# Layer-0 projections as two column tiles of 64 channels, and a new order of a unit's steps, in a two-layer attention kernel

## The chip, the cores and the metric

The kernel runs on one core of a Trainium2 chip. The metric is the device time of one execution in microseconds (us). Before the change the median of three runs is 2491.27 us, with 2487.93 us the lowest and 2491.57 us the highest. About 0.2% (5 us) is what a measurement of this kernel can tell from no change.

## The reference

`x` has shape (8, 512, 32, 32): 8 images, 512 channels, 1024 tokens, all float32. Layer 0 is a group norm, eight-head attention over the 1024 tokens and an output projection with a residual. Layer 1 projects to values, attends among the 256 tokens of greatest norm and writes these back before its own output projection. The change touches layer 0 alone, whose core is:

```
h    = group_norm(x, gn_w, gn_b).reshape(B, C, N)
qkv  = einsum('oc,bcn->bon', qkv_w, h) + qkv_b        # q, k, v: 8 heads x 64 channels
attn = softmax(einsum('bhdi,bhdj->bhij', q, k) * 64**-0.5)
out  = einsum('bhij,bhdj->bhdi', attn, v).reshape(B, C, N)
x1   = x + einsum('oc,bcn->bon', proj_w, out) + proj_b
```

## The kernel before

**Units.** Layer 0 works in 64 units: a unit `t` is one pair of heads (`p = t // 2`, of 4 pairs per image) and one half of the query tokens (`hf = t % 2`, 512 of 1024). In a unit, keys go in eight blocks `j` of 128. `scores` (L947) multiplies q and k for both heads: each head has a contraction of 64 channels, so the two heads stand in the two row halves of the TensorE array and run at the same time. The raw scores are copied to SBUF by ScalarE (`keep`, L955); VectorE follows the maximum (`highest`, L961), turns it into one number per query (`turn`, `negate`), which goes out to DRAM and comes back spread over all partitions (`nb`); ScalarE puts that into PSUM (`spread`, L1002), VectorE adds it (`shift`, L1006), ScalarE takes the exponential (L1009), GpSimd sums the eight exponentials (`add`, L1014), and `values` (L1022) multiplies by v. In `values` each head gives 64 output channels, so the two heads stand in the two *column* halves of the array. `total` (L1037) sums over partitions in four column tiles of 32; `take` (L1045) copies, `invert` (L1051) takes the reciprocal, which again goes through DRAM, and `divide` (L1064) scales the unit's output.

**Fills.** Between these steps stand up to five "fills" per unit: other matrix products of 8 or 16 TensorE passes that go through one PSUM bank (pool `ps_g`, one buffer), each emptied by an "empty" before the next fill may start. Fills 0 and 1 project q or k of a later pair (L750), fill 2 projects v (L771), fills 3 and 4 are the output projection of the image before (L789), in four units of each image from the second on. `side(t)` lists them. All of these use the whole 128 x 128 array.

**Order.** Every engine works its instructions in the order written. The order inside a unit is the word list `SLOT`, read word by word by the loop at the end of `layer0`: a name and number is a step and its block; each `+` means that the step belongs to the next unit, each `-` to the one before. So one pass of the loop holds steps of up to four units. `FIRST_STEPS` places the first products before the loop is full; the last entries of `side` place the start of layer 1 among the last units; `norms` hangs the next image's group norm on certain words of `SLOT`.

**Buffers that tie the order.** Scores and `total` share two PSUM buffers (`ps_s`), so a score product waits until the one two before it has been copied and compared. The product with v has one buffer (`ps_a`): the first `values` step of a unit waits for `divide` of the unit before. Exponentials go through 14 buffers (`ep`).

A float32 product is two TensorE passes for each matmul of the program, so a fill of four matmuls shows as eight in the trace.

Of the kernel before, what the change touches and what calls it, by code (L numbers as in the profile page):

```python
# [18 lines left out]
P = 128  # L19
B = 8  # L20
C = 512
N = 1024
CT = C // P
NB = N // P
NH = 2
HALF = N // NH
HEADS = 8
HD = 64
NPAIR = HEADS // 2
# [16 lines left out]


SLOT = """
fill1 max5+ sc3+ spread empty1 max2+ sub1 exp1 sub0 sub2 sc6+ fill0 exp0 keep3+ div- val1 sub5
add1 max3+ val0 exp2 max6+ exp5 val2 sub6 add2 empty0 keep6+ sub3 val5 sub7 exp6 fill3+ add5  # L50
sc4+ exp3 sub4 empty3+ add6 exp7 sc7+ max4+ exp4 keep4+ add3 max7+ fill2+ keep7+ turn+ neg+
sc0++ add7 sc1++ val3 keep0++ val6 val4 val7 keep1++ add4 den max1++ empty2+ fill4 take inv
sc5++ sc2++ keep5++ empty4 keep2++
"""


# [62 lines left out]
def attention_then_topk_attention(  # L119
# [18 lines left out]
    nc = tc.nc  # L138
# [469 lines left out]
    def layer0():  # L608
        with ExitStack() as st:
# [19 lines left out]
            hs = {0: load_x(0)}  # L629
# [27 lines left out]
            vs, qs, ks, os = {}, {}, {}, {}  # L657
# [73 lines left out]
            def norms(t, name, j):  # L731
                for b in {t // (NPAIR * NH) + 1, (t + 4) // (NPAIR * NH) + 1}:
                    at = t - (b - 1) * NPAIR * NH
                    if 0 < b < B:
# [3 lines left out]
                        for step, *which in todo:  # L738
                            step(b, *which)


            def project(p, which, hf):

                b, hp = divmod(p, NPAIR)
                all_ = (qs, ks)[which]
                ot = which * CT + hp

                def fill(pq):
                    for k in range(CT):
                        nc.tensor.matmul(  # L750
                            pq, wqkv[:, k, ts(ot, P)], hs[b][:, k, ts(hf, HALF)],
                            start=(k == 0), stop=(k == CT - 1),
                        )

                def empty(pq):
                    if p not in all_:
                        all_[p] = qk_tile("qk"[which], p % 2, f"{'qk'[which]}_{p}")
                    nc.scalar.activation(
                        all_[p][:, ts(hf, HALF)], pq, AF.Identity, bias=bqkv[:, ot : ot + 1],
                    )  # L760

                return fill, empty

            def v_tokens(m, part):

                b, hm = divmod(m, NPAIR // 2)

                def fill(pv):
                    for j in range(2):
                        for k in range(CT):  # L770
                            nc.tensor.matmul(  # L771
                                pv[:, ts(j, 2 * P)], hs[b][:, k, ts(2 * part + j, P)],
                                wqkv[:, k, 2 * C + hm * 2 * P : 2 * C + (hm + 1) * 2 * P],
                                start=(k == 0), stop=(k == CT - 1),
                            )

                def empty(pv):
                    if part == 0:
                        vs[m] = vp.tile([P, NB, 2 * P], F32, tag="v", name=f"v_{m}")
                    nc.scalar.copy(  # L780
                        vs[m][:, ts(part, 2), :], pv.rearrange("p (a c) -> p a c", c=2 * P)
                    )

                return fill, empty

            def project_out(b, mt, hf):
                def fill(po):
                    for k in range(CT):
                        nc.tensor.matmul(  # L789
                            po, wp[:, k, ts(mt, P)], os[b * NPAIR + k][:, ts(hf, HALF)],  # L790
                            start=(k == 0), stop=(k == CT - 1),
                        )

                def empty(po):
                    xr = resid.pop((b, mt, hf))
                    nc.vector.scalar_tensor_tensor(
                        xr, po, pb[:, mt : mt + 1], xr, ALU.add, ALU.add,
                    )
                    nc.sync.dma_start(x1_dram[b][:, mt, ts(hf, HALF)], xr)

                return fill, empty
# [39 lines left out]
            def side(t):  # L841

                todo = []
                p, hf = divmod(t, NH)
                b, at = divmod(t, NPAIR * NH)
                m, part = divmod(t, 2 * NH)
                if hf == 0 and p + 1 < PAIRS:
                    todo += [project(p + 1, 1, h) for h in (1, 0)]
                if hf == 1 and p + 2 < PAIRS:
                    todo += [project(p + 2, 0, h) for h in (1, 0)]  # L850
                if m + 1 < PAIRS // 2:
                    todo.append(v_tokens(m + 1, part))
                if b and 1 <= at <= CT:
                    todo += [project_out(b - 1, at - 1, h) for h in range(NH)]
                if t == 0:
                    todo[2:] = [v_tokens(0, 1), project(1, 0, 0), project(1, 0, 1)]
                if t == 1:
                    todo.append(v_tokens(1, 0))
                if 2 <= t <= 3:
                    todo.append((bias_row, bias_columns)[t - 2]())  # L860

                if t == UNITS - 4:
                    todo.insert(2, turned_values(0))
                if t == UNITS - 3:
                    todo = [joint(0), turned_values(3), turned_values(2), turned_values(1), joint(3)]
                if t == UNITS - 2:
                    todo = [token_values(1), token_values(0), joint(2), joint(1), token_rows(0)]
                if t == UNITS - 1:
                    todo = [
                        token_rows(1), token_values(4), token_values(3), token_values(2),  # L870
                        project_out(B - 1, 0, 0),
                    ]
                return todo

# [294 lines left out]
            with tc.manual_schedule(engines=ORDERED):  # L1169
                for c in range(CT):  # L1170
                    norm_stats(0, c)
                mean_sum(0, ps_g.tile([P, HALF], F32, tag="g", name="pm_0"))
                mean_take(0)
                spread_of(0)
                variance_sum(0, ps_g.tile([P, HALF], F32, tag="g", name="pv_0"))
                variance_take(0)
                norm_factors(0)
                for c in range(CT):
                    norm_apply(0, c)

                FIRST_STEPS = {
                    (-2, "sc", 1): [v_tokens(0, 0)],
                    (-2, "sc", 2): ["empty", project(0, 0, 1)],
                    (-1, "sc", 6): ["empty", v_tokens(0, 2)],
                    (-1, "sc", 7): ["empty"],
                    (-1, "empty", 2): [v_tokens(0, 3)],
                    (-1, "keep", 2): ["empty"],
                }
                pending = []

                def first(step):
                    if step == "empty":
                        end, pt = pending.pop(0)
                        end(pt)
                    else:
                        pool, tag = ((ps_g, "g"), (ps_a, "av"))[len(firsts) % 2]
                        firsts.append(step)
                        pt = pool.tile([P, HALF], F32, tag=tag, name=f"first_{len(firsts)}")
                        step[0](pt)
                        pending.append((step[1], pt))  # L1200

                firsts = []
                for step in (
                    project(0, 1, 0), project(0, 0, 0), "empty", project(0, 1, 1), "empty", "empty",
                ):
                    first(step)
                for t in range(-max(ahead for _, ahead, _ in order), UNITS + 1):
                    if t == -2:
                        hs[1] = load_x(1)
                    if t == 2:  # L1210
                        constants()
                    for name, ahead, j in order:
                        late = name in ("den", "take", "inv", "div") and t + ahead == UNITS - 1
                        if 0 <= t + ahead < UNITS and not late:
                            STEPS[name](t + ahead, j)
                        for step in FIRST_STEPS.get((t, name, j), []):
                            first(step)
                        norms(t, name, j)
                        if name == "div":
                            loads(t)  # L1220
                        if t == UNITS - 1 and (name, j) == ("fill", 1):
                            also(token_rows(2))
                    if t == UNITS - 1:
                        begin_layer1()
                finish()
# [48 lines left out]
```

## Time and profile before

| | |
|---|---|
| median of the runs | 2491.27 us |
| the profiled execution's own time | 2489.56 us |
| its span (first to last instruction) | 2487.9 us |
| TensorE (PE) busy | 2437.7 us, 98% |
| VectorE (DVE) busy | 1963.3 us, 79% |
| ScalarE (ACT) busy | 1414.8 us, 57% |
| GpSimd (POOL) busy | 1160.7 us, 47% |
| mean granted TensorE clock | 0.999 |

Busy TensorE time is the union of its passes, whose ends are modelled; a pass overlaps the next one's start. So what a pass costs is read from the distance of two starts, not from its duration. The weight loads (PEld) run beside the passes. Layer 0 fills the first 2020 us of the span, layer 1 the rest.

### The profile page before, as it was taken

The numbers are of one execution on the slowest core, as the hardware profiler recorded it, in microseconds if no ns is written. First come the engines' busy times: TensorE is split into PE (matmuls) and PEld (weight loads), VectorE is DVE, ScalarE is ACT, GpSimd is POOL, SyncE is SP. The second block draws the span as 40 slices with busy tenths as digits, with TensorE's granted clock in tenths as the row PEclk, the third lists the DMA queues.
The fourth block names the chain that finished last, engine by engine and source line by source line (L and its number), as shares of the span: only waits on it lengthen the run. The fifth ranks groups of instructions, "written<-read, shape, count | busy, mean of one in ns | idle before, by whom it ended". The sixth has DMA issues, their size and how long they took to land. (4 is left out here: it accounts for less than half of the span.)

```text
span 2487.9 us, 27088 instructions
## 1 busy us (share of the span) xinstructions
PE 2437.7 (98%) x9164; PEld 1076.4 (43%) x9164; DVE 1963.3 (79%) x2946; ACT 1414.8 (57%) x1828; POOL 1160.7 (47%) x557
## 2 busy tenths in 40 slices
PE   7999999999999999999999999999999999999998
PEld 3434444444444444444444444444433345555554
DVE  4789987998898889888988898888777566666683
ACT  2567755665666566655765676567656533333421
POOL 0555644665465555545664565455555501111122
PEclk9999999999999999999999999999999999999999
DMA  3002011111211121112011201111213343566553
GB/s 142 15 26 73 30 56 51 69 35 56 84 31 43 56 79 41 43 60 77 26 47 56 77 26 49 59 39 35 89 52 106 123 161 136 209 211 240 188 198 106
DMA packets 108234, 205.24 MB, mean 82 GB/s; under 512 B 19114, under 2 KB 19370, under 8 KB 108096
## 3 DMA queue, kind: packets, MB, share of 16 engines
q1 hardware_dynamic: 82432, 159.95, 19.0%
q10 hardware_dynamic: 18144, 31.48, 3.4%
q0 software_dynamic: 7520, 12.09, 1.7%
q8 instruction: 72, 1.18, 0.2%
q14 instruction: 66, 0.54, 0.1%
HBM read 146.29 MB, written 69.73 MB: 87 GB/s over the span
## 5 line engine op out<-in xcount | busy, mean ns | idle before, releaser
L1014 POOL TENSOR_TENSOR es<-es,e 128x1024 f32<-128x1024 f32 x384 | 912.0, 2375 | 30.1
L955 ACT COPY e<-sc 128x1024 f32<-128x1024 f32 x512 | 505.6, 1013 | 389.4 <-PE sc L947 241.3
L1006 DVE TENSOR_TENSOR e<-e,ns 128x1024 f32<-128x1024 f32 x512 | 594.0, 1212 | 2.0 <-ACT ns L1002 2.0
L1014 POOL TENSOR_TENSOR es<-e,e 128x1024 f32<-128x1024 f32 x64 | 152.0, 2375 | 884.8 <-ACT e L1009 884.8
L1009 ACT ACTIVATE e<-e 128x1024 f32<-128x1024 f32 x512 | 529.1, 1055 | 31.6 <-DVE e L1006 9.8
L961 DVE TENSOR_TENSOR high<-sc,high 128x1024 f32<-128x1024 f32 x384 | 468.9, 1221 | 90.0 <-ACT e L955 50.3
L947 PE MATMUL sc<-q,k 64*128 64x512 f32 x2048 | 510.4, 616 | 5.3 <-ACT e L955 3.2
L1022 PE MATMUL av<-e,v 128*64 128x512 f32 x2048 | 469.4, 600 | 3.5 <-ACT e L1009 2.0
L750 PE MATMUL g<-x,wqkv 128*128 128x512 f32 x992 | 458.8, 605 | 3.4 <-ACT v L780 1.7
L947 PEld LDWEIGHTS sc<-q,k 64*128 64x128 f32 x2048 | 175.3, 185 | 283.6 <-issue 151.3
L750 PEld LDWEIGHTS g<-x,wqkv 128*128 128x128 f32 x992 | 178.3, 189 | 274.8 <-issue 229.9
L1022 PEld LDWEIGHTS av<-e,v 128*64 128x64 f32 x2048 | 136.1, 137 | 320.6 <-issue 257.5
L771 PE MATMUL g<-wqkv,x 128*128 128x256 f32 x976 | 227.0, 386 | 1.3 <-DVE pb L834 1.3
L789 PE MATMUL g<-o,wp 128*128 128x512 f32 x456 | 210.9, 605 | 0.8
L771 PEld LDWEIGHTS g<-wqkv,x 128*128 128x128 f32 x976 | 180.4, 190 | 69.7 <-issue 43.3
L1051 DVE RECIPROCAL rs<-rs 128x256 f32<-128x256 f32 x64 | 112.1, 1751 | 68.4 <-ACT rs L1045 68.4
L534 POOL DMA_INDIRECT V<-sa,at x64 | 64.2, 1003 | 155.2 <-DMA sa<-att 52.7
L789 PEld LDWEIGHTS g<-o,wp 128*128 128x128 f32 x456 | 81.9, 189 | 118.2 <-issue 91.3
L309 PE MATMUL b_pv<-w,x 128*128 128x512 f32 x256 | 114.1, 592 | 0.0
L405 PE MATMUL b_pp<-w,selT 128*128 128x512 f32 x256 | 112.5, 593 | 0.8 <-ACT selT L396 0.7
L961 DVE TENSOR_TENSOR high<-sc,e 128x1024 f32<-128x1024 f32 x64 | 78.1, 1220 | 37.5 <-ACT e L955 37.5
L363 POOL DMA_INDIRECT sel<-sx,who x16 | 16.1, 1007 | 191.0 <-DMA out_dram<-y 72.1
(177 smaller groups left out, 1993.6 us busy)
## 6 DMA issues: line engine op xcount, KB each, us to landing
nb<-negd SPq DMA_DIRECT2D x128, 256.0 KB
x<-in_x_dram SPq DMA_DIRECT2D x32, 512.0 KB
ri<-rsd SPq DMA_DIRECT2D x128, 128.0 KB
sx<-xT ACTq DMA_DIRECT2D x64, 256.0 KB
xr<-in_x_dram SPq DMA_DIRECT2D x58, 256.0 KB
x1d<-xr SPq DMA_DIRECT2D x58, 256.0 KB
sv<-V ACTq DMA_DIRECT2D x56, 256.0 KB
y<-x1d SPq DMA_DIRECT2D x48, 256.0 KB
```

The source lines that it names most:

```text
L309: nc.tensor.matmul(pv, x1[b][k][:, ts(j, P)], w["vo"][:, k, :], start=(k == 0), stop=(k == CT - 1),)
L405: nc.tensor.matmul(pp, tiles["selT", b][:, k, ts(rb, P)], w["qk"[which]][:, k, :], start=(k == 0), stop=(k == CT - 1),)
L750: nc.tensor.matmul(pq, wqkv[:, k, ts(ot, P)], hs[b][:, k, ts(hf, HALF)], start=(k == 0), stop=(k == CT - 1),)
L771: nc.tensor.matmul(pv[:, ts(j, 2 * P)], hs[b][:, k, ts(2 * part + j, P)], wqkv[:, k, 2 * C + hm * 2 * P : 2 * C + (hm + 1) * 2 * P], start ...
L789: nc.tensor.matmul(po, wp[:, k, ts(mt, P)], os[b * NPAIR + k][:, ts(hf, HALF)], start=(k == 0), stop=(k == CT - 1),)
L947: nc.tensor.matmul(sc[:, hh, :], ks[p][r, ts(j, P)], qs[p][r, ts(hf, HALF)], start=True, stop=True,)
L955: nc.scalar.copy(raw[t, j], banks["s", t, j])
L961: nc.vector.tensor_tensor(high[t], banks["s", t, j], raw[t, 0] if j == 1 else high[t], ALU.max)
L1006: nc.vector.tensor_tensor(raw[t, j], raw[t, j], high[t], ALU.add)
L1009: nc.scalar.activation(raw[t, j], raw[t, j], AF.Exp, scale=QK_SCALE)
L1014: nc.gpsimd.tensor_add(sums[t], raw[t, 0] if j == 1 else sums[t], raw[t, j])
L1022: nc.tensor.matmul(avs[t][HD * hh : HD * hh + HD, :], vs[p // 2][:, j, (p % 2) * P + HD * hh : (p % 2) * P + HD * hh + HD], e[:, hh, :], s ...
```

## The change

1. A helper `product` replaces the plain matmul in `project`, `v_tokens` and `project_out`. It issues each product twice, once for output channels (rows of the PSUM bank) 0 to 63 and once for 64 to 127, with 64 columns of weights each. The moving operand and the sums are the same; the number of matmul and weight-load instructions of these three doubles. The array is then used as two column tiles of 64, as `values` uses it.
2. The order of the steps in a unit (`SLOT`) is another one. Two of the eight `values` steps (blocks 3 and 4) move into the next pass of the loop, right behind fill 1; the others stand behind fill 0 (blocks 5, 0, 1) and after the score products of blocks 3 and 4 (blocks 2, 7, 6). Fill 4 moves from behind `total` to ahead of the `values` steps 2, 7 and 6; fill 2 moves to just ahead of `total`.
3. The entries of `side` for the first and the last three units, and `FIRST_STEPS`, are rearranged to suit.

```diff
 SLOT = """
-fill1 max5+ sc3+ spread empty1 max2+ sub1 exp1 sub0 sub2 sc6+ fill0 exp0 keep3+ div- val1 sub5
-add1 max3+ val0 exp2 max6+ exp5 val2 sub6 add2 empty0 keep6+ sub3 val5 sub7 exp6 fill3+ add5
-sc4+ exp3 sub4 empty3+ add6 exp7 sc7+ max4+ exp4 keep4+ add3 max7+ fill2+ keep7+ turn+ neg+
-sc0++ add7 sc1++ val3 keep0++ val6 val4 val7 keep1++ add4 den max1++ empty2+ fill4 take inv
-sc5++ sc2++ keep5++ empty4 keep2++
+fill1 max5+ keep2+ max2+ spread val3- val4- sc7+ empty1 sub0 sub1 exp0 sub5 exp1 sc6+ exp5 
+sub4 fill0 div- val5 exp4 add1 add4 max6+ sub2 keep7+ max7+ empty0 sub7 sub6 exp2 val0 keep6+ 
+exp7 sub3 val1 fill3+ empty3+ sc3+ sc4+ add5 fill4 add2 val2 exp6 max3+ val7 keep3+ max4+ add6 
+turn+ add7 keep4+ neg+ val6 exp3 sc0++ empty4 add3 keep0++ sc1++ fill2 max1++ den keep1++ take 
+empty2 inv sc5++ sc2++ keep5++
 """
...
+            def product(out, wide_, moving, k):
+                for r in (slice(0, HD), slice(HD, P)):
+                    nc.tensor.matmul(
+                        out[r, :], wide_[:, r], moving, start=(k == 0), stop=(k == CT - 1),
+                    )
...
                     for k in range(CT):
-                        nc.tensor.matmul(
-                            pq, wqkv[:, k, ts(ot, P)], hs[b][:, k, ts(hf, HALF)],
-                            start=(k == 0), stop=(k == CT - 1),
-                        )
+                        product(pq, wqkv[:, k, ts(ot, P)], hs[b][:, k, ts(hf, HALF)], k)
...
-                            nc.tensor.matmul(
+                            product(
                                 pv[:, ts(j, 2 * P)], hs[b][:, k, ts(2 * part + j, P)],
-                                wqkv[:, k, 2 * C + hm * 2 * P : 2 * C + (hm + 1) * 2 * P],
-                                start=(k == 0), stop=(k == CT - 1),
+                                wqkv[:, k, 2 * C + hm * 2 * P : 2 * C + (hm + 1) * 2 * P], k,
                             )
...
-                        nc.tensor.matmul(
-                            po, wp[:, k, ts(mt, P)], os[b * NPAIR + k][:, ts(hf, HALF)],
-                            start=(k == 0), stop=(k == CT - 1),
-                        )
+                        product(po, wp[:, k, ts(mt, P)], os[b * NPAIR + k][:, ts(hf, HALF)], k)
...
                 if t == 0:
-                    todo[2:] = [v_tokens(0, 1), project(1, 0, 0), project(1, 0, 1)]
+                    todo[2:] = [project(1, 0, 1), project(1, 0, 0)]
...
                 if t == UNITS - 3:
-                    todo = [joint(0), turned_values(3), turned_values(2), turned_values(1), joint(3)]
+                    todo = [turned_values(3), turned_values(2), joint(2), turned_values(1), joint(1)]
                 if t == UNITS - 2:
-                    todo = [token_values(1), token_values(0), joint(2), joint(1), token_rows(0)]
+                    todo = [token_values(0), joint(3), token_values(2), joint(0), token_rows(0)]
                 if t == UNITS - 1:
                     todo = [
-                        token_rows(1), token_values(4), token_values(3), token_values(2),
-                        project_out(B - 1, 0, 0),
+                        token_values(3), token_rows(1), project_out(B - 1, 0, 0),
+                        token_values(1), token_values(4),
                     ]
...
                     (-2, "sc", 2): ["empty", project(0, 0, 1)],
-                    (-1, "sc", 6): ["empty", v_tokens(0, 2)],
-                    (-1, "sc", 7): ["empty"],
-                    (-1, "empty", 2): [v_tokens(0, 3)],
-                    (-1, "keep", 2): ["empty"],
+                    (-1, "sc", 7): ["empty", v_tokens(0, 2)],
+                    (-1, "sc", 6): ["empty", v_tokens(0, 1)],
+                    (-1, "keep", 7): ["empty"],
+                    (-1, "sc", 4): [v_tokens(0, 3)],
+                    (-1, "turn", 0): ["empty"],
```

## The prediction

> **What bounds the kernel now.** First the busy times and the 40 slices of the span:
>
> ```profile
> PE 2437.7 (98%) x9164; PEld 1076.4 (43%) x9164; DVE 1963.3 (79%) x2946; ACT 1414.8 (57%) x1828; POOL 1160.7 (47%) x557
> ...
> PE   7999999999999999999999999999999999999998
> ...
> DVE  4789987998898889888988898888777566666683
> ...
> PEclk9999999999999999999999999999999999999999
> ```
>
> TensorE has work in every slice at the full clock; VectorE comes close to full in layer 0. Busy time does not say whether the passes follow each other as fast as they can, so I read next the timeline of PE inside one unit of image 4 (columns: start, length, what):
>
> ```profile
> 1202.45 1.99 PE L947 MATMUL sc<-q,k 64*128 64x512 f32 x8
> 1204.36 3.70 PE L750 MATMUL g<-x,wqkv 128*128 128x512 f32 x8
> 1207.99 1.99 PE L947 MATMUL sc<-q,k 64*128 64x512 f32 x8
> 1209.91 3.70 PE L750 MATMUL g<-x,wqkv 128*128 128x512 f32 x8
> 1213.54 3.65 PE L1022 MATMUL av<-e,v 128*64 128x512 f32 x16
> 1217.13 1.99 PE L947 MATMUL sc<-q,k 64*128 64x512 f32 x8
> 1219.04 3.72 PE L771 MATMUL g<-wqkv,x 128*128 128x256 f32 x16
> ```
>
> No row has a bracket for idle time. Now the pitch of single passes, from the weight loads beside them:
>
> ```profile
> 1205.33 0.19 PEld L750 LDWEIGHTS g<-x,wqkv 128*128 128x128 f32 x1 [0.24 <-issue]
> 1205.76 0.19 PEld L750 LDWEIGHTS g<-x,wqkv 128*128 128x128 f32 x1 [0.24 <-issue]
> 1206.19 0.19 PEld L750 LDWEIGHTS g<-x,wqkv 128*128 128x128 f32 x1 [0.24 <-issue]
> ...
> 1214.45 0.14 PEld L1022 LDWEIGHTS av<-e,v 128*64 128x64 f32 x2 [0.29 <-issue]
> 1214.88 0.14 PEld L1022 LDWEIGHTS av<-e,v 128*64 128x64 f32 x2 [0.29 <-issue]
> ```
>
> One pass of 512 columns every 0.43 us, and a *pair* of half-width passes also every 0.43 us: half the width costs nothing when the other half works beside it. Eight passes at 0.429 are 3.43 us, but the fill takes 3.63 from its start to the next start (1204.36 to 1207.99). Likewise four row pairs are 1.72 and take 1.91; eight column pairs are 3.43 and take 3.59; 16 passes of 256 columns (0.2155 each) are 3.45 and take 3.65. So each change of the array's shape costs 0.20 us for full and row shapes, 0.155 for the column shape. Where two fills follow each other, the cost is absent:
>
> ```profile
> 43.23 3.72 PE L771 MATMUL first<-wqkv,x 128*128 128x256 f32 x16
> 46.79 3.60 PE L750 MATMUL g<-x,wqkv 128*128 128x512 f32 x8
> 50.31 1.99 PE L947 MATMUL sc<-q,k 64*128 64x512 f32 x8
> ```
>
> 46.79 to 50.31 is 3.52 and 43.23 to 46.79 is 3.56: together 0.20 less than with a change between. The bound is the sum of TensorE passes and shape changes.
>
> **The change: TensorE.** Fills take the column shape, so they join the `values` steps without a change. In the built programs' order of instructions I counted runs of one shape: before 276 full, 256 row, 127 column, 64 of `total`; after 36 full, 256, 260 and 64. Hence 240 fewer at 0.20 = −48.0 us, 133 more at 0.155 = +20.6, sum **−27.4 us**.
>
> By unit: a unit without fills 3 and 4 has before 4 x 1.91 (scores) + 2 x 3.63 + 3.65 (fills) + 2 x 3.59 (values) + 0.57 (`total`, 1201.88 to 1202.45) = 26.3 us. After: four row runs 7.64; fill 1 with two value steps, 12 x 0.429 + 0.155 = 5.30; fill 0 with three, 14 x 0.429 + 0.155 = 6.16; three value steps 2.73; fill 2 16 x 0.2155 + 0.155 = 3.60; `total` 0.57; sum 26.0. Each fill 3 or 4 saves 0.20 more, as it joins a run that exists anyway.
>
> **Twice the instructions.** The fills have 2,560 passes (L750 and L771 1,024 each, L789 512); 2,560 come on top. The Trainium skill, "TensorEngine Tiling (Array Packing)", section Instruction Overhead, gives each matmul some 60 cycles; at the 2.4 GHz of "TensorE: Matmul & The Clock Gate" that is an estimate of 25 ns x 2,560 = +64 us, and the change would lose 37. The row says otherwise: 16 half-width passes take 3.65, 8 full ones 3.70. I take the row: nothing. Its limit is that a fill of v has passes of 256 columns, and half-width pairs of that length stand nowhere in the trace. Both loads of a pair must fit into 0.2155 us. Lower end: they overlap, as above (two in 0.14), cost 0. Upper end: one after the other, 2 x 0.137 = 0.274, or +0.0585 a pair; 1,024 pairs make +60. The nearest row is `total`, 8 passes of 256 in four column tiles in 0.57, which leaves 0.14 beyond two pitches; so overlap, 0. The issue rate asked is four instructions in 0.2155, 54 ns each; transposes do it:
>
> ```profile
> 2466.39 2.18 PE b_po L550 x20
> ```
>
> 20 passes with 20 loads in 2.18 us, 54 ns an instruction.
>
> **The change: order.** A shorter TensorE unit is a gain only if the other engines keep up. The tightest loop in the timeline of all engines: `total` at D; copy D+0.70; reciprocal D+1.11; two maxima; two shifts; two exponentials; first sum on GpSimd at D+8.93 (1210.81 − 1201.88); seven sums, last end at 1227.88, 17.07 later; then the next `total`. At its closest,
>
> ```profile
> 186.72 0.64 PE L1037 MATMUL den<-es,ones 128*32 128x256 f32 x8 [0.16 <-POOL es L1014]
> ```
>
> it starts 0.05 after the last sum. The loop is 8.93 + 17.07 + 0.05 = **26.05 us**; before it had 0.27 to spare under 26.32, after it ends together with TensorE's 26.0. The new word list keeps the loop's steps (max5, max2, two shifts, empty1 ahead of both exponentials); whether exponential 0 or 1 comes first does not matter, as the sum needs both. The 22 or so units without fills 3 and 4 in full flow thus get 0.05 less: +1 us. With fills 3 or 4 a unit has 29 us and more, and the loop is slack.
>
> The other waits, by summing rows along each engine's new order from D (fill 1 starts at D+2.55):
> - `negate` ends at D+23.8 (VectorE: reciprocal to 2.86, then 7 maxima and 8 shifts at 1.13, `divide` 0.6, turn and negate 4.05). The longest return of the spread maximum is 6.9 (1226.27 to 1233.15, ScalarE's second copy), plus 0.6 to copy: 31.3, or 5.2 after the next D. The first shift wants it at D+5.31. It fits by 0.1; each us late costs a us in these 22 units.
> - `divide` is due at D+9.8, the reciprocal is back within 6.2 of D+2.86: 0.8 spare. The queue of SP has the same transfers in the same sequence.
> - One PSUM bank for fills: fill 0 starts at D+9.7, ScalarE empties fill 1 at D+6.8; fill 4, 1.9 after fill 3, waits for VectorE's empty3, which by then has nothing before it; the next fill 1 has 0.9 spare.
> - Score buffers: block 4's product wants `keep6` done, 0.8 spare; block 2's wants `take`, 0.4 spare.
> - VectorE works 24.65 of a 26.32 us unit, so 26.05 still holds it. The values of blocks 3 and 4, a pass later, have their exponentials long done.
>
> Start and end: before, TensorE waits there some 7 and 11 us (bracketed idle times from 55 to 187 us and from 1880 to 2021). The new lists make other waits; bounds −5 and +5, taken 0.
>
> Sum: −27.4 + 1 = −26.4 on the profiled execution's 2489.56 (span 2487.9), i.e. 2463.2. The median shown is 1.7 above that execution; I forecast **2463**.
>
> **Rivals.**
> 1. *The new order loses a cover.* The return of the maximum or an exponential comes 0.5 us late in the 22 units: +11, **2474**. For: 0.1 spare. Against: in the old order the same return decided nothing though it was later against D. Chance 13%.
> 2. *Half-length pairs do not keep pitch* in the fills of v, the slower side: 2463 + 60 = **2523**; from +0.026 us a pair (0.241 instead of 0.2155) it eats the whole gain. For: no such row. Against: the loads overlap, `total` runs. Chance 12%, with smaller losses in between.
> 3. *The change doesn't do what it says:* a fill and a `values` step differ in operands, and the join costs 0.155 like a change. 188 such joins in the new order: +29, **2492**. Against: L771 to L750 above. Chance 6%.
>
> **How the numbers follow.** The forecast has 69%; its own range is 2455 to 2472 (start and end ±5, shape changes ±10%, loop). With rival 1 the range is **2450 to 2482**; rivals 2 and 3 stay outside, 18%. Faster by over 0.2% (5 us): 69 + 13 = 82%. Within 0.2%: 5%, rival 3. Slower: 13%.
>
> **What would show it.** Right: L744 with 256 columns at 3.45 to 3.60 a fill, starts of `total` 26.05 apart, no bracket between a fill and `values`. Rival 1: idle brackets of `total` behind POOL, and POOL's first sum later than D+8.93. Rival 2: a pair pitch over 0.22 in the fill of v. Rival 3: a 0.15 step where fill and values meet. The forecast is wrong if TensorE's starts have idle time of over 10 us between 190 and 1880 us.

## The result, and the profile after

The changed kernel takes 2459.41 us (median of four runs, 2458.73 to 2460.64); the kernel before, on the same chip, 2490.64 us (2487.93 to 2491.57). The ratio is 0.9877, with a 95% interval of 0.986 to 0.9894: faster by 1.2%, 31 us. The forecast was 2463 us.

The busy times and slices of the changed kernel's page, to set beside those of before:

```profile
PE 2410.3 (98%) x11724; PEld 967.2 (39%) x11724; DVE 1949.5 (79%) x2946; ACT 1405.2 (57%) x1828; POOL 1162.9 (47%) x557
...
PE   7999999999999999999999999999999999999998
...
DVE  4899988988898889888988897889777466666683
...
PEclk9999999999999999999999999999999999999999
```

TensorE has 2,560 passes more and is busy 27 us less. Its share is 98% as before: a shorter kernel with the same bound. The timeline of PE in the changed kernel, from one `total` to the next, in a unit without fills 3 and 4 (start, length, what):

```profile
1178.37 0.64 PE L1037 MATMUL den<-es,ones 128*32 128x256 f32 x8
1178.94 1.99 PE L947 MATMUL sc<-q,k 64*128 64x512 f32 x8
1180.86 3.65 PE L744 MATMUL g<-x,wqkv 128*64 128x512 f32 x16
1184.34 1.89 PE L1022 MATMUL av<-e,v 128*64 128x512 f32 x8
1186.16 1.99 PE L947 MATMUL sc<-q,k 64*128 64x512 f32 x8
1188.08 3.65 PE L744 MATMUL g<-x,wqkv 128*64 128x512 f32 x16
1191.56 2.74 PE L1022 MATMUL av<-e,v 128*64 128x512 f32 x12
1194.23 1.99 PE L947 MATMUL sc<-q,k 64*128 64x512 f32 x8
1196.15 2.80 PE L1022 MATMUL av<-e,v 128*64 128x512 f32 x12
1198.88 1.99 PE L947 MATMUL sc<-q,k 64*128 64x512 f32 x8
1200.80 3.67 PE L744 MATMUL g<-wqkv,x 128*64 128x256 f32 x32
1204.42 0.64 PE L1037 MATMUL den<-es,ones 128*32 128x256 f32 x8
```

Read it by the distance of starts. Fill 1 and the two value steps behind it go from 1180.86 to 1186.16: 5.30 us, of which 12 pitches of 0.429 are 5.15, and one change of shape is the rest. Fill 0 and three value steps: 6.15. Three value steps: 2.73. The fill of v, 32 half-width passes of 256 columns: 3.62. From `total` to `total` it is 26.05 us, where it was 26.32.

Between them stand GpSimd's sums of this unit, the first started by the exponentials (the bracket), the last ended at 1204.37:

```profile
1187.27 2.38 POOL L1014 TENSOR_TENSOR es<-e,e 128x1024 f32<-128x1024 f32 x1 [8.95 <-ACT e L1009]
1189.73 14.64 POOL L1014 TENSOR_TENSOR es<-es,e 128x1024 f32<-128x1024 f32 x6
```

The next `total` starts 0.05 us behind the last sum.

Where the time went, by the starts of `total` in both traces: from the eighth to the 56th (six images in full flow) 1443.8 us became 1420.5, −23.3. The start of the kernel up to the eighth `total` became 8.1 shorter (292.0 to 283.9). But 5.2 of these are work that the new order only puts behind that `total`: two value steps (four pitches of 0.429) and one fill of v (before the eighth `total` there are 12 of them, where there were 13; 16 pitches of 0.2155). That leaves 2.9. From the 56th `total` to the first product of layer 1 it is 0.2 longer with these 5.2, so 5.0 shorter without them. Layer 1 differs by 0.3.

### The profile page after: what moved, and what is told of

It is laid out like the page before. It is cut to its first block, busy times and chain, and to the rows that moved or that the text cites. A ratio compares the mean times of both kernels' runs of the same rounds, so it can differ in the third digit from the quotient of the medians.

```text
span 2457.0 us, 32002 instructions
## 1 busy us (share of the span) xinstructions
PE 2410.3 (98%) x11724; PEld 967.2 (39%) x11724; DVE 1949.5 (79%) x2946; ACT 1405.2 (57%) x1828; POOL 1162.9 (47%) x557
## 5 line engine op out<-in xcount | busy, mean ns | idle before, releaser
L1022 PE MATMUL av<-e,v 128*64 128x512 f32 x2048 | 476.2, 596 | 4.6 <-DVE o L1064 3.2
L744 PE MATMUL g<-x,wqkv 128*64 128x512 f32 x1984 | 453.1, 598 | 0.7 <-ACT v L783 0.7
L1022 PEld LDWEIGHTS av<-e,v 128*64 128x64 f32 x2048 | 144.2, 137 | 303.8 <-issue 285.4
L744 PEld LDWEIGHTS g<-x,wqkv 128*64 128x64 f32 x1984 | 131.3, 136 | 306.9 <-issue 292.1
L744 PE MATMUL g<-wqkv,x 128*64 128x256 f32 x1920 | 220.4, 382 | 0.0
L744 PE MATMUL g<-o,wp 128*64 128x512 f32 x912 | 207.0, 595 | 0.0
L744 PEld LDWEIGHTS g<-wqkv,x 128*64 128x64 f32 x1920 | 132.5, 137 | 106.0 <-issue 34.7
L744 PEld LDWEIGHTS g<-o,wp 128*64 128x64 f32 x912 | 64.4, 137 | 134.1 <-issue 117.9
```

What stands on the lines that cost most here:

```text
L744: nc.tensor.matmul(out[r, :], wide_[:, r], moving, start=(k == 0), stop=(k == CT - 1),)
L1022: nc.tensor.matmul(avs[t][HD * hh : HD * hh + HD, :], vs[p // 2][:, j, (p % 2) * P + HD * hh : (p % 2) * P + HD * hh + HD], e[:, hh, :], s ...
```

## Experiments

Each run has the kernel before beside it on the same chip; that one's median moved between 2490.6 and 2495.2 us from chip to chip, so ratios are to be compared, or kernels of one group. The last column is read from one trace of each kernel: where the first product of layer 1 starts (2020.7 before the change). Layer 1, which none of these edits touches, takes 465.9 to 472.4 us in the traces, so this start is a steadier measure of layer 0; in the two traces of the changed kernel it is 1989.5 and 1988.9.

| kernel | median, us | before, us | ratio | 95% interval | layer 1 starts, us |
|---|---|---|---|---|---|
| the change | 2459.41 | 2490.64 | 0.9877 | 0.986 to 0.9894 | 1989.5 |
| shape_alone | 2472.37 | 2493.18 | 0.9914 | 0.99 to 0.9927 | 2000.6 |
| order_alone | 2494.25 | 2493.18 | 1.0003 | 0.9995 to 1.0011 | 2024.4 |
| v_on_full_array | 2462.83 | 2493.18 | 0.9881 | 0.9866 to 0.9896 | 1988.5 |
| four_tiles_of_32 | 2478.1 | 2493.18 | 0.994 | 0.9925 to 0.9956 | 2005.7 |
| changed_again | 2462.1 | 2491.85 | 0.9879 | 0.9863 to 0.9896 | 1988.9 |
| norm_sums_in_columns | 2457.04 | 2491.85 | 0.9858 | 0.9842 to 0.9875 | 1985.9 |
| all_layer0_in_columns | 2456.42 | 2491.85 | 0.9864 | 0.9847 to 0.988 | 1984.4 |
| half_of_v | 2406.57 | 2491.45 | 0.9658 | 0.963 to 0.9686 | 1937.5 |
| half_of_v_six_sums | 2392.12 | 2491.45 | 0.96 | 0.9566 to 0.9634 | 1921.2 |
| shape_and_fill4_ahead | 2529.95 | 2495.18 | 1.0141 | 1.0124 to 1.0158 | 2058.3 |
| shape_fill4_empty4_ahead | 2480.66 | 2491.33 | 0.9957 | 0.9943 to 0.997 | 2011.6 |

### The two halves of the change, each by itself

`shape_alone` is the kernel before with `product` in the three projections; `order_alone` is the changed kernel with

```diff
-                for r in (slice(0, HD), slice(HD, P)):
-                    nc.tensor.matmul(
-                        out[r, :], wide_[:, r], moving, start=(k == 0), stop=(k == CT - 1),
-                    )
+                nc.tensor.matmul(out, wide_, moving, start=(k == 0), stop=(k == CT - 1))
```

> The kernel before with only the first part of the change: the fills of q, k, v and the output projection as two column tiles of 64, in the old order of steps. Theory (each change of the array's shape costs 0.20 us for full and row runs, 0.155 for column runs, and a fill beside a values step joins it for nothing): the program has 34 full, 284 column, 256 row and 64 total runs against 276, 127, 256 and 64, so -242 x 0.20 + 157 x 0.155 = -24 us, about 2467 us. Rival, the order is what gains: 2491 us. Rival, doubling the instructions costs something that the new order hides: over 2467, up to 2491.

> The changed kernel with the fills back on the whole 128 x 128 array, in the new order of steps. Theory: the order sets fills beside values steps, which now differ in shape, so there are 265 full, 192 column, 256 row and 64 total runs against 276, 127, 256, 64 before: -11 x 0.20 + 65 x 0.155 = +8 us, less the 4 us of idle time that the new order saves at both ends: 2495 us, slower than before. Rival, the order is what gains: about 2463 us.

Measured: `shape_alone` takes 21 us less than the kernel before, and `order_alone` does not differ (1 us more; in its trace layer 0 is 3.7 longer). So the shape is what gains. The order by itself gains nothing: it sets fills beside value steps that do not have their shape. PE of `order_alone`, timeline:

```profile
1201.96 3.70 PE L743 MATMUL g<-x,wqkv 128*128 128x512 f32 x8
1205.59 1.94 PE L1019 MATMUL av<-e,v 128*64 128x512 f32 x8
1207.46 1.99 PE L944 MATMUL sc<-q,k 64*128 64x512 f32 x8
```

Fill and two value steps take 3.63 + 1.87 = 5.50 here, 5.30 in the changed kernel: the 0.2 of the missing join. Both runs fell some 3 us from their expectation, in opposite directions: `shape_alone` gained 3 less, `order_alone` lost 3 less.

That 21 and −1 do not add up to 31 is for the most part the count itself: shape changes give −24 and +8 apart, but −27.4 together. What the count does not give is how much the order adds to the shape: 10 us, where the count gives 3 (638 runs of one shape in `shape_alone`, 616 in the changed kernel). In the traces the six images in full flow take 7.2 us less than in `shape_alone`, of which the count gives 3.7; some 3 more lie at the end of layer 0. In full flow the trace of `shape_alone` shows two places. The first is a unit of 33.75 us, where the next one, with the same fills, takes 33.04 (33.79 and 33.58 before the change). It waits twice, for the emptying of fill 4 and for a copy of scores, and its scores start late:

```profile
349.43 0.64 PE L1039 MATMUL den<-es,ones 128*32 128x256 f32 x8
...
355.75 3.65 PE L745 MATMUL g<-x,wqkv 128*64 128x512 f32 x16 [0.18 <-DVE xr L798]
...
378.53 1.13 PE L949 MATMUL sc<-q,k 64*128 64x512 f32 x4 [0.18 <-ACT e L957]
...
383.18 0.64 PE L1039 MATMUL den<-es,ones 128*32 128x256 f32 x8
```

The second is a unit in which fill 4 stands between `total` and the next scores. PE and POOL around it:

```profile
416.22 0.64 PE L1039 MATMUL den<-es,ones 128*32 128x256 f32 x8
...
446.07 0.64 PE L1039 MATMUL den<-es,ones 128*32 128x256 f32 x8
```

```profile
428.89 2.40 POOL L1016 TENSOR_TENSOR es<-e,e 128x1024 f32<-128x1024 f32 x1 [15.63 <-ACT e L1011]
431.37 14.65 POOL L1016 TENSOR_TENSOR es<-es,e 128x1024 f32<-128x1024 f32 x6
```

The first sum starts 12.67 us after `total` (8.90 in the changed kernel), the last ends at 446.02, and `total` follows 0.05 later: the loop over GpSimd binds a unit of 29.85 us, where TensorE's work would need 29.6 (26.0, eight pitches of 0.429 and one change of shape of 0.155). Fill 4 stands ahead of the scores and fill 1 behind `total`, and so delays the exponentials. In the changed kernel fill 4 stands ahead of the value steps, and such a unit takes 29.46.

### Is that move alone the rest?

This kernel is `shape_alone` with one more change, the place of fill 4 in the word list:

```diff
-sc0++ add7 sc1++ val3 keep0++ val6 val4 val7 keep1++ add4 den max1++ empty2+ fill4 take inv
+sc0++ add7 sc1++ val3 keep0++ val6 val4 val7 keep1++ add4 empty2+ fill4 den max1++ take inv
```

> The old order with the column shape (as shape_alone), and in the word list one move alone: fill 4 from behind total to ahead of it, right behind the values steps (with the empty of fill 2 ahead of it, as both use one PSUM bank). In shape_alone fill 4 stands between total and the next scores: the first sum on GpSimd then starts at D+12.66 instead of D+8.90, and the loop binds units of 29.85 and 29.65 us (last sum to total 0.06 us), which need 29.5. Theory (what the new order adds is that move): fill 4 joins the values steps, 610 runs instead of 638, -4.3 us, and two units of an image are freed by 0.2 to 0.4 us, -4 us: some 8 us less than shape_alone, 29 us under before, about the changed kernel. Rival (the value steps of blocks 3 and 4 in the next pass, or the rest of the word list, bring the remainder): 4 us less than shape_alone or nothing.

Measured: 2529.95 us, 35 us *slower* than the kernel before the change. The move was incomplete. PE, timeline:

```profile
358.87 5.35 PE L745 MATMUL g<-x,wqkv 128*64 128x512 f32 x16 [3.77 <-DVE xr L798]
```

Fill 1 waits 3.77 us for the emptying of fill 4, which stood on VectorE behind the reciprocal of the next `total`. With one bank for all fills, a fill has to be moved together with its empty. So the next kernel has also `empty4` ahead of `take inv`:

> As shape_and_fill4_ahead, and the empty of fill 4 moved with it: on VectorE from behind the reciprocal to ahead of it. In the run before, fill 1 stood 3.77 us idle behind that empty (DVE xr), since both use the one PSUM bank and VectorE came to it only after the reciprocal of the next total. Theory as there: without that wait the move brings some 8 us against shape_alone, so 29 us under before (ratio 0.988). Rival: the remainder of the new order is needed: not under shape_alone's ratio of 0.991 by more than 0.002.

Measured: ratio 0.9957, 11 us under the kernel before and 10 us worse than `shape_alone`. So the theory, that this move is what the order adds, is wrong: the unit of 29.85 us that the loop had bound became 29.46 as expected, but others now wait: three of an image take 34.13, 33.80 and 27.0 us, where the changed kernel has 33.13, 32.90 and 26.05. PE of that kernel, the waits from 300 to 450 us:

```profile
358.33 1.13 PE L949 MATMUL sc<-q,k 64*128 64x512 f32 x4 [0.70 <-DVE high L963]
359.66 1.13 PE L949 MATMUL sc<-q,k 64*128 64x512 f32 x4 [0.20 <-DVE high L963]
415.84 3.65 PE L745 MATMUL g<-o,wp 128*64 128x512 f32 x16 [0.69 <-ACT v L785]
```

Scores wait for the maxima on VectorE, and fill 4 for the copy of fill 2 on ScalarE. The new order gives more than this one move. Which of its other words are needed was not tried one by one and stays open.

### Is it the joins, or the column shape, or the number of instructions?

`v_on_full_array` puts the fill of v alone back on the whole array; `four_tiles_of_32` replaces the halves by quarters:

```diff
-                for r in (slice(0, HD), slice(HD, P)):
+                for r in (slice(g * P // 4, (g + 1) * P // 4) for g in range(4)):
```

> The changed kernel with only the fill of v back on the whole array. It stands between score products and total, so it joins nothing: 87 full and 198 column runs against 36 and 260, sum +0.5 us. Theory: 2460 us, the same as the changed kernel; the whole gain comes from fills that stand beside values steps. Rival, half-length pairs of passes lose pitch: this is faster than the changed kernel, by up to 60 us. Rival, column shape is in itself faster for fills: slower by some 10 us or more.

> The changed kernel with each product of a fill in four column tiles of 32 channels, so twice the instructions again, and a shape that values does not share. Theory (shape changes alone count, the number of instructions does not): runs 36 full, 192 column of 64, 266 column of 32, 256 row, cost 125.4 us against 107.7, so +18 us, about 2477 us. Rival, the instruction count costs (25 ns each for 5,120 more): +128 us and more, about 2590 us; the fill of v would show it first, as it asks for eight instructions in 0.2155 us, 27 ns each.

The 25 ns of the last rival are the estimate that the prediction works out from 60 cycles a matmul, and names the source of. Measured: `v_on_full_array` has 0.9881 against 0.9877 for the change, the same; `four_tiles_of_32` is 15 us under the kernel before, where 13.5 (2490.6 to 2477) was expected. So the fill of v gains nothing that can be measured, having no neighbour of its shape, and quarters lose half of the gain because `values` does not share their shape. The number of instructions costs nothing here. PE of `four_tiles_of_32`, timeline:

```profile
1209.98 3.66 PE L744 MATMUL g<-wqkv,x 128*32 128x256 f32 x64
1213.46 0.61 PE L1037 MATMUL den<-es,ones 128*32 128x256 f32 x8
```

64 passes and 64 weight loads in 3.48 us, 27 ns an instruction, where 16 pitches of 0.2155 are 3.45. Here `total` follows without a change of shape, since it too uses tiles of 32.

### What bounds a unit now

`half_of_v` leaves out half of the passes of fill 2 (`for k in (0, CT - 1)` in `v_tokens`); `half_of_v_six_sums` leaves out one GpSimd sum too (`if j == 3: return` in `add`). Both therefore compute something else; they only serve to find the bound. Each was run twice.

> The changed kernel with two of the four channel blocks of every product for v left out, so half of TensorE's passes of fill 2 (8 pitches of 0.2155 = 1.72 us a unit, 64 units) are gone; v is then computed from half of its channels. If TensorE bounds all units: -110 us, about 2349 us. Theory (the loop of total, reciprocal, maxima, shifts, exponentials and GpSimd's seven sums takes 26.05 us and bounds the 22 units without fills 3 and 4): those units stay at 26.05 from one total to the next, the other 42 lose 1.72 each: -72 us, about 2387 us, with TensorE idle ahead of total behind POOL.

> As the one before, with the sum of block 3's exponentials on GpSimd left out too, so six sums in place of seven (the denominator lacks an eighth). Theory: the loop falls by 2.45 us to 23.6, so the 22 units become free to follow TensorE at 26.0 - 1.72 = 24.3 us between two totals, if VectorE's 24.65 us of work lets them: 24.3 to 25, and the run falls by another 22 x 1.1 to 1.7 = 24 to 38 us, about 2355 us. Rival (something other than the sums held the units at 26.05): no further change.

Measured: 2406.57 and 2392.12 us. PE of `half_of_v`, the waits ahead of `total`:

```profile
1169.39 0.64 PE L1037 MATMUL den<-es,ones 128*32 128x256 f32 x8 [1.68 <-POOL es L1014]
1195.41 0.64 PE L1037 MATMUL den<-es,ones 128*32 128x256 f32 x8 [1.65 <-POOL es L1014]
```

The distance is 26.02 with 1.72 us of TensorE work gone, and the idle time behind POOL is that 1.7: in units without fills 3 and 4 nothing more is to be had from TensorE. That part of the theory is shown. The size was 20 us off: I had 42 units losing 1.72 each. Of the eight of an image three stayed at 26.0 to 26.3 and five lost 1.0 to 1.7 (29.78, 33.21, 33.13, 32.90, 29.46 became 28.05, 32.26, 31.40, 31.40, 27.97), 7.0 us an image for 8.6. That is 10 us in six images; the other 10 lie in the start and the end, whose 12 units lost 10 us together and not 21.

With six sums the loop is 2.45 us shorter, but the run fell by 14 us only, not by 24 to 38. Of the three units without fills 3 and 4 in an image one came down to 24.54, as expected; two fell only from 26.03 to 25.58, and the unit behind them rose from 28.05 to 29.33. VectorE of `half_of_v_six_sums` in a unit of 25.58 (`total` at 931.00):

```profile
930.49 1.20 DVE L961 TENSOR_TENSOR high<-sc,e 128x1024 f32<-128x1024 f32 x1
931.62 1.26 DVE L666 BATCH_NORM_STATS2 bs<-x 128x6 f32<-128x512 f32 x2
932.92 0.21 DVE L667 BATCH_NORM_AGGREGATE mv<-bs 128x2 f32<-128x12 f32 x1
933.10 1.75 DVE L1053 RECIPROCAL rs<-rs 128x256 f32<-128x256 f32 x1
935.14 2.55 DVE L961 TENSOR_TENSOR high<-sc,high 128x1024 f32<-128x1024 f32 x2 [0.29 <-ACT e L955]
```

The reciprocal has no bracket: it follows the statistics back to back and starts 2.1 us after `total` instead of 1.11. VectorE is busy for 24.8 of the 25.58 us and has 0.29 of bracketed idle time, so I read it as the bound now; no run took work from it to show that. So three bounds stand within half a us: TensorE 26.0, the loop over GpSimd 26.05, VectorE 25.6.

### More of the same

`norm_sums_in_columns` gives the column shape to the 14 products of 128 x 4 ahead of `total` too; `all_layer0_in_columns` also to `joint` and `token_values`.

```diff
-                nc.tensor.matmul(pm[:, :CT], gmat, gns[b][:, :, 0], start=True, stop=True)
+                halves(pm[:, :CT], gmat, gns[b][:, :, 0])
...
+            def halves(out, wide_, moving, first=True, last=True):
+                for r in (slice(0, HD), slice(HD, P)):
+                    nc.tensor.matmul(out[r, :], wide_[:, r], moving, start=first, stop=last)
```

> The changed kernel itself, as the measure for the two beside it on the same chip: 31 us under the kernel before, as in its own comparison.

> The changed kernel with the 14 little products of the group norm (mean_sum, variance_sum, 128 x 4) ahead of total also as two column tiles of 64, so that they join the fill of v: 21 full runs instead of 36, sum -15 x 0.20 = -3.0 us against the changed kernel. Theory of shape changes: 3 us less than the changed kernel beside it. Rival, the loop over GpSimd's sums binds there too: no difference.

> As the one before, and the products at the end of layer 0 that prepare layer 1 (joint, token_values) as two column tiles of 64 too: 12 full runs, 592 runs in all against 616, sum -4.8 us against the changed kernel, if the end of layer 0 is bound by TensorE; there it waits for other engines in part, so -3 to -5 us.

Measured: 2462.1, 2457.04 and 2456.42 us. The runs of the first two do not overlap (2461.28 to 2462.96; 2453.67 to 2458.16): 5 us less than the changed kernel, where 3 were expected. The timeline of PE, first in the changed kernel, then with the sums in columns:

```profile
309.73 3.67 PE L744 MATMUL g<-wqkv,x 128*64 128x256 f32 x32
313.33 0.39 PE L671 MATMUL den<-mv,gmat 128*128 128x4 f32 x2
313.65 0.64 PE L1037 MATMUL den<-es,ones 128*32 128x256 f32 x8
```

```profile
309.34 3.67 PE L748 MATMUL g<-wqkv,x 128*64 128x256 f32 x32
312.85 0.23 PE L663 MATMUL den<-mv,gmat 128*64 128x4 f32 x4
313.01 0.64 PE L1041 MATMUL den<-es,ones 128*32 128x256 f32 x8
```

From the fill to `total` 3.92 became 3.67, 0.25 in each of 14 places, 3.5 us by the rows. In the two traces layer 1 starts 3.0 us earlier, as expected; layer 1 itself, which the edit does not touch, differs by 3.9, so what goes beyond 3 is not the edit's. The second addition, at the end of layer 0, brings nothing that the runs can tell apart (2454.91 to 2461.05); in its one trace layer 1 starts 4.5 us earlier than in the changed kernel, where 4.8 was expected.

## Why the prediction was right

- **The bound.** TensorE's passes and shape changes set the time: right. The units in full flow fell by 23.3 us over six images; by the prediction's units it is 24.0 less 0.05 in each of 18, 23.1. The idle time of TensorE's starts from 190 to 1880 us is 5.1 us; over 10 would have spoken against the forecast.
- **The price of a change of shape**, 0.20 and 0.155: right. The sums for the runs were 5.30, 6.16, 2.73, 3.60 and 0.57; the trace has 5.30, 6.15, 2.73, 3.62 and 0.57. A column run costs its entry once, however many fills and steps are in it. The Trainium skill's "TensorEngine Tiling (Array Packing)", section Key Properties, says that changing the mode, not just the tile, drains the array; the traces here give the price and agree that a change of tile in one mode costs nothing.
- **Doubled instructions at nothing:** right, and with room: even quarters keep pitch, 64 passes in 3.48 us. The 60 cycles that the Trainium skill's "TensorEngine Tiling (Array Packing)", section Instruction Overhead, gives a matmul would have made the change lose if they were added to each, as the prediction's estimate of +64 us did; nothing was added here. The section goes on that a free dimension of 1 takes as long as one of 60, which reads as a floor under short products; the fills here have 256 or 512 columns, and no run tests the floor.
- **Half-length pairs**, the slower rival: excluded by the 3.62 us of the fill of v, and by `v_on_full_array`.
- **The loop of 26.05 us:** right. The first sum starts 8.90 us behind `total`, and the next `total` 0.05 after the last. `half_of_v` shows that it binds by itself.
- **The other waits:** the returns and copies that I found to fit by 0.1 to 0.9 us did fit in full flow, but for 0.2 us in one unit of each image (33.13 for 32.90). The tightest sum has a slip that did no harm: it lists seven maxima ahead of `negate`, which would end at 24.5 behind `total`. The trace has six, and `negate` ends at 23.86, where 23.8 was forecast.
- **Start and end**, taken as 0 within −5 to +5: this is the term that was off. With the shifted work taken out, the start is 2.9 and the end 5.0 us shorter, where the rest of the sum (−26.4 less −23.1) leaves 3.3 for both. That is 4.6 us more than forecast and the difference between 2463 and 2459. Counting the runs of one shape in the two traces stretch by stretch puts it at the end: they give −2.8 for the start, which is what it lost, and −1.3 for the end, which lost 3.7 more. 1.5 of these are less bracketed idle time (12.4 to 10.9 us). Which entry of the new lists brought it was not tried. It lay inside the stated ±5, but nothing in the prediction foresaw its sign.
- **The order.** The prediction counted it only through the joins. It adds ten of the 31 us to what the shape gains by itself, seven more than the count gives. The forecast of the whole did not suffer, as it summed the finished unit and compared it with the loop. A forecast of the shape alone by the same count was 3 us too good: in the old order fill 4 lengthens the loop and makes scores and fill 1 wait, which I had not looked for there.

## What to carry to other kernels

Where products of different shapes alternate on TensorE, count the changes of array shape: here each cost 0.15 to 0.20 us, and a full-width product split into column tiles loses nothing and can stand beside a product that uses those tiles anyway. The order decides how many joins there are: here the shape paid 21 us without the new order, the order nothing without the shape, and both 31. Before a TensorE saving is booked, sum the loop through the other engines from one fixed point back to itself: here it lay 0.27 us under the unit and took over as soon as the unit had lost 0.3.

## What was not expected of the hardware

In `four_tiles_of_32` products in four column tiles of 32, with passes of 256 columns, ran at 27 ns an instruction (64 passes and 64 weight loads in 3.48 us) without losing pitch.
